# A gated delta rule on one core: the state as the stationary operand, keys and queries as the moving one, and a turn back by transposition

## The chip, the cores and the metric

The kernel runs on one core of a Trainium2 chip. The metric is the device time of one execution in microseconds. Three timed runs of the kernel before gave 3100.2, 3089.31 and 3093.5 us; their median is 3093.5 us. One more execution was taken with the hardware profiler. It took 3072.88 us, of which the profile's span covers 3071.2 us, so that 1.7 us lie around the span. All durations below come from this profiled execution.

## What is computed

The reference is a sequence of two blocks over x of shape 8 x 512 x 256, all in float32: a gated recurrence with an MLP, a mixture of experts (8 experts, top 2, and a shared one), then the layer that the change touches, and last an attention over the half of the tokens that a router chooses. The layer that matters is a gated delta rule with 8 heads, keys of 128 and values of 64:

```python
def step(state, inp):                       # state: batch, head, 64 values, 128 keys
    q_t, k_t, v_t, a_t, b_t = inp
    retained = jnp.einsum('bhvk,bhk->bhv', state, k_t)
    ...
    state = a4 * (state - b4 * rk) + b4 * vk
    o_t = jnp.einsum('bhvk,bhk->bhv', state, q_t)
    return (state, o_t)
```

Before this step come projections of x, a causal convolution of width 4, a SiLU and a normalization of q and k; behind it a gated RMS norm and a projection.

## The kernel before

The kernel runs its stages one behind the other: the first block, the experts, the delta rule, the attention. The function `delta_rule` does the third. It doesn't step through the 512 tokens one by one. For each batch element (8) and each half of the heads (`hg`, 0 or 1, four heads each) it forms a **group**; there are 16 groups, and each treats its 512 tokens in four blocks (`t`) of 128. Inside a block the recurrence is a triangular system; `prepare` (L918, L920) forms its matrices, `inverses` (L948 to L1058) inverts them for a whole group in place, and only the state between blocks is carried on by steps in order.

These steps are the generator `advance`. For the blocks t = 1, 2, 3 of a group, that is 48 times in all, it first reads the old state with the keys and the queries of the block (L1122, tile `pkq`), scales the result by the decay on VectorE (L1124, tile `old`) and takes the part for the keys from the right side `r` (L1125). Then, for every block: `pw` (L1129) applies the inverse to `r`, ScalarE copies it to `w` (L1131), `pst` (L1140) makes the update of the state, which VectorE adds (L1144), and `pow` (L1148) gives what goes into the output `o` (L1152). The tile `state` holds 128 keys on the partitions and 4 heads x 64 values; `kq` holds 128 key channels on the partitions, and for each head the 512 tokens of k and then of q.

In L1122 the operand that is loaded into the array (stationary) is a 128 x 128 piece of `kq`, and the one that streams through it (moving) is the 128 x 64 state of a head. There are 2 x 4 such products in a step. In float32 each product is two instructions on TensorE, each with a weight load of its own.

A group isn't done alone. While group n is advanced, the matrices of group n+1 are formed and inverted, the channels of group n+2 are projected, convolved and normalized (`channels` L848 to L853, `norms` L866 to L885, `fade` L896 to L903), the gates of group n are made (`silus`, L1096 to L1098), a later batch element is loaded (`load`), and the result of group n is normed and projected (`outputs`, L1160 to L1181). Each of these is a generator, and the string `order` says whose next piece is written down: `a` is `advance`, `p` is `prepare`, `i` is `inverses`, `c` is `channels`, `g` is `silus`, and so on. From what is written down in this order, the tile framework's scheduler settles the order of the instructions on each engine. On the chip each engine goes through its own list in that order and waits where an operand isn't there.

The accumulation tiles of `advance` (`pkq`, `pw`, `pst`, `pow`) share the PSUM pool `pq` with two buffers. `old` has two buffers in the pool `un`.

Two places of `inverses` stand near the end of a group's advance and matter below. VectorE ends the inversion of the small blocks with `inv`; ScalarE copies it to `cols` (L986); VectorE transposes that to `dn` (L935); TensorE makes `pn` from it (L1003, 64 products of 32 x 32 blocks); VectorE turns `pn` into `join` (L1004); and TensorE makes `pd` of `join` and `up` (L1009), from which the rest of the inversion follows. These lines belong to the next group, but stand on the same engines.

Of the kernel before, what the change touches and what calls it, by code (L numbers as in the profile page):

```python
# [14 lines left out]
F32 = mybir.dt.float32  # L15
# [5 lines left out]
P = 128  # L21
# [10 lines left out]
H1, VD = 8, 64  # L32
HG = 4
# [4 lines left out]
def bc(ap, axis, n):  # L38

    ap = ap.unsqueeze(axis)  # L40
    shape = list(ap.shape)
    shape[axis] = n
    return ap.to_broadcast(shape)
# [3 lines left out]
def block(ctx: ExitStack, tc: tile.TileContext, a: dict, out: bass.AP):  # L47
    nc = tc.nc
    V, S, G, TE = nc.vector, nc.scalar, nc.gpsimd, nc.tensor
# [4 lines left out]
    def cst(shape, name):  # L54
        return const.tile(shape, F32, name=name, tag=name)

    ident = cst([P, P], "ident")
# [708 lines left out]
    def delta_rule():  # L766
        with ExitStack() as cx:
# [334 lines left out]
            def advance(s):  # L1102


                b, hg, hs, dec, NQ = s.b, s.hg, s.hs, s.dec, s.NQ
                state = None
                for t in range(NT):
                    ts = slice(t * P, (t + 1) * P)
                    r = s.r[t]

                    def sv(tag, **kw):
                        return un.tile([P, HG, VD], F32, name=f"{tag}{b}_{hg}_{t}", tag=tag, **kw)

                    def ps_sv(what):
                        return pq.tile([P, HG, VD], F32, name=f"{what}{b}_{hg}_{t}", tag="pq")

                    old = None
                    if state is not None:
                        ps = pq.tile([P, 2, HG, VD], F32, name=f"pkq{b}_{hg}_{t}", tag="pq")
                        for n in range(2):  # L1120
                            for h in range(HG):
                                TE.matmul(ps[:, n, h, :], s.kq[:, h, n, ts], state[:, h, :], start=True, stop=True)  # L1122
                        old = un.tile([P, 2, HG, VD], F32, name=f"old{b}_{hg}_{t}", tag="old")
                        V.tensor_mul(old, ps, bc(bc(dec[:, 0, t, hs], 1, 2), 3, VD))  # L1124
                        V.tensor_sub(r, r, old[:, 0, :, :])  # L1125
                        yield
                    ps = ps_sv("pw")
                    for h in range(HG):
                        TE.matmul(ps[:, h, :], NQ[:, 0, t * HG + h, :], r[:, h, :], start=True, stop=True)  # L1129
                    w = sv("w")  # L1130
                    S.copy(w, ps)  # L1131
                    yield
                    new = None
                    if t < NT - 1:
                        new = sv("state")
                        if state is not None:
                            G.tensor_mul(new, state, bc(dec[:, 2, t, hs], 2, VD))
                        ps = ps_sv("pst")
                        for h in range(HG):
                            TE.matmul(ps[:, h, :], s.K[t][:, h, :], w[:, h, :], start=True, stop=True)  # L1140
                        if state is None:
                            V.tensor_copy(new, ps)
                        else:
                            V.tensor_add(new, new, ps)  # L1144
                        yield
                    ps = ps_sv("pow")
                    for h in range(HG):
                        TE.matmul(ps[:, h, :], NQ[:, 1, t * HG + h, :], w[:, h, :], start=True, stop=True)  # L1148
                    if state is None:
                        S.activation(s.o[:, t, :, :], ps, AF.Copy, scale=-1.0)  # L1150
                    else:
                        V.tensor_sub(s.o[:, t, :, :], old[:, 1, :, :], ps)  # L1152
                    yield
                    state = new
# [73 lines left out]
            def group(n):  # L1228
# [6 lines left out]


            order = """
                p v t p v p l a v p t l a v p a p a p l a p a p a i l a i g a i c l g i a a e i l a g i e c i a a i l e g e
                i c o i l c o c i o c i l c o i o c i o l i c o i i c o n o n c c n
            """.split()  # L1240

            def seats():
# [44 lines left out]
            with ExitStack() as px:  # L1287
# [5 lines left out]
                for k in first:  # L1293
                    if k not in work:
                        if k in "76":
                            work[k] = shared(next(left), sht, pp, po)
                        elif k in "cneCNE":
                            n = 0 if k in "cne" else 1
# [18 lines left out]
            un = late[0] = cx.enter_context(tc.tile_pool(name="c_un", bufs=2, side="right", reuse_waits="tile"))  # L1317
            pt_ = cx.enter_context(tc.tile_pool(name="c_pt", bufs=2, space=PSUM, reuse_waits="tile"))
            pq = cx.enter_context(tc.tile_pool(name="c_pq", bufs=2, space=PSUM, reuse_waits="tile"))
# [7 lines left out]
            for n in range(total):  # L1327
                s, s1 = groups.pop(n), groups.get(n + 1)
                work = {"v": sides(s), "g": silus(s), "a": advance(s), "o": outputs(s)}
                if s1 is not None:  # L1330
                    work |= {"p": prepare(s1), "i": inverses(s1)}
                if n % 2 == 0 and coming is not None:
                    work["t"] = coming
                elif n + 3 < total:
                    work["l"] = coming = load(n // 2 + 2)
                else:
                    coming = None
                for k in order:
                    if k in "cne" and n + 2 < total and k not in work:
                        if "t" in work:  # L1340
                            drain(work["t"])
                        if n + 2 not in groups:
                            groups[n + 2] = group(n + 2)
                        work[k] = {"c": channels, "n": norms, "e": fade}[k](groups[n + 2])
                    if k in work:
                        next(work[k], None)
                        if n >= total - 2 and k != "p" and groups_done(work, n):
                            steps_ += 1
                            if steps_ % 3:
                                next(sitting, None)  # L1350
                work.pop("l", None)
                drain(*work.values())
            drain(sitting)

    delta_rule()
    kept.close()

# [268 lines left out]
```

## Time and profile before

| what | us |
|---|---|
| median of three timed runs | 3093.5 |
| the profiled execution | 3072.88 |
| its span | 3071.2 |
| TensorE busy in the span | 2884.1 |
| VectorE busy | 1850.4 |
| ScalarE busy | 1587.0 |
| first `pkq` to last `pkq` | 1572.5 to 2722.5 |
| from one group's first `pkq` to the next one's, mean of the 15 distances | 75.0 |

A busy share says how long an engine had an instruction in work. For TensorE it is too high, since products follow each other in a pipeline and the ends are modelled; the time from the start of one instruction to the start of the next is the better measure. The chain of work that ended last follows the time back from the last instruction through what released each one; its shares say which engine set the end. The windows view gives the busy time of every engine in stretches of time, and the timeline lists instructions in order, with the idle time before each and what ended it in square brackets.

### The profile page before, as it was taken

How to read it: one execution, taken by the hardware profiler on the slowest of the kernel's cores; microseconds unless marked ns; L12 is line 12 of the kernel's file. 1: busy time of each engine (PE TensorE's matmuls, PEld its weight loads, DVE VectorE, ACT ScalarE, POOL GpSimd, SP SyncE). 2: the span in 40 equal slices, each digit the busy share in tenths (PEclk: the TensorE clock that was granted, in tenths of full speed). 3: DMA queues.
4: the chain of work that ended last, by engine and by line, in shares of the span. 5: the costliest groups of instructions: out<-in, count | busy, mean ns of one | idle time of the engine just before them, and what ended most of it. 6: DMA issues, size and time to landing. Idle time of an engine off the chain costs nothing.

```text
span 3071.2 us, 59437 instructions
## 1 busy us (share of the span) xinstructions
PE 2884.1 (94%) x24598; PEld 2140.5 (70%) x24598; DVE 1850.4 (60%) x4322; ACT 1587.0 (52%) x2839; POOL 534.1 (17%) x653
## 2 busy tenths in 40 slices
PE   7999999999999999998899999999999999869997
PEld 4565556557999999995466666666666666756774
DVE  5555554545555555556756778687877776654442
ACT  4545453222333333334666677777777776744432
POOL 1000000530100100103111212121212111341111
PEclk9999999999999999999999999999999999769997
DMA  1500001524888888882000001000000000131112
GB/s 69 171 14 28 14 7 26 200 70 152 326 335 331 326 327 331 326 308 76 15 9 1 27 4 29 2 29 2 29 2 26 2 9 22 41 109 57 44 37 66
DMA packets 101406, 307.15 MB, mean 100 GB/s; under 512 B 12680, under 2 KB 83728, under 8 KB 91920
## 3 DMA queue, kind: packets, MB, share of 16 engines
q0 software_dynamic: 19440, 221.19, 19.0%
q1 hardware_dynamic: 79776, 79.80, 7.8%
q8 instruction: 193, 3.16, 0.4%
q10 hardware_dynamic: 1920, 2.37, 0.2%
q14 instruction: 77, 0.63, 0.1%
HBM read 253.25 MB, written 50.08 MB: 99 GB/s over the span
## 4 chain that ended last, share of the span: by engine, by line
PE 74%; DVE 11%; DMA 5%; issue 5%; ACT 4%; POOL 2%; POOLq 0%; DVEq 0%; ACTq 0%
PE p_r L492 15%; PE pc L848 6%; PE p_s L492 5%; PE pp L336 4%; PE pyr L650 4%; PE pj L443 4%; PE pk L918 3%; PE pf L437 3%; DMA w<-in_experts,wrow 3%; PE pkq L1122 2%; DVE cy L852 2%; PE st L1500 2%; PE py L1180 2%; PE pys L535 1%; PE sc L1479 1%
## 5 line engine op out<-in xcount | busy, mean ns | idle before, releaser
L492 PE MATMUL p_r<-zT,w 128*128 128x128 f32 x4544 | 533.3, 275 | 5.4 <-DMA w<-in_experts,wrow 4.8
L492 PEld LDWEIGHTS p_r<-zT,w 128*128 128x128 f32 x4544 | 525.2, 192 | 11.0 <-issue 6.2
L852 DVE SCALAR_TENSOR_TENSOR cy<-pc,conv,cy 128x511 f32<-128x511 f32 (+2 forms) x480 | 351.9, 741 | 137.9 <-ACT cy L850 133.9
L496 ACT ACTIVATE t_r<-p_r,w 128x128 f32<-128x128 f32 x568 | 171.1, 374 | 266.8 <-PE p_r L492 177.0
L492 PE MATMUL p_s<-sxT,shared_w 128*128 128x512 f32 x512 | 231.3, 604 | 3.4 <-ACT sxT L132 1.2
L497 DVE SCALAR_TENSOR_TENSOR l_r<-p_r,w,t_r 128x128 f32<-128x128 f32 x284 | 79.9, 344 | 178.7 <-PE p_r L492 178.7
L492 PEld LDWEIGHTS p_s<-sxT,shared_w 128*128 128x128 f32 x512 | 97.1, 193 | 120.5 <-issue 98.7
L632 POOL DMA_INDIRECT w<-in_experts,wrow x71 | 67.0, 944 | 654.4 <-ACT sg_r L505 634.2
L848 PE MATMUL pc<-cxT,wq 128*128 128x512 f32 x256 | 145.7, 690 | 2.8 <-DVE cy L852 2.5
L336 PE MATMUL pp<-hT,win 128*128 128x512 f32 x320 | 145.6, 609 | 0.1
L497 DVE SCALAR_TENSOR_TENSOR g_r<-p_r,w,t_r 128x128 f32<-128x128 f32 x284 | 80.0, 344 | 98.6 <-PE p_r L492 98.6
L1481 DVE TENSOR_REDUCE maxs<-sc 128x2 f32<-128x512 f32 x128 | 79.4, 683 | 99.0 <-PE sc L1479 99.0
L650 PE MATMUL pyr<-w,htr 128*128 128x256 f32 x568 | 135.5, 382 | 2.1 <-DVE htr L510 2.1
L850 ACT ACTIVATE cy<-pc,conv 128x512 f32<-128x512 f32 x160 | 108.7, 685 | 43.4 <-PE pc L848 41.2
L848 PE MATMUL pc<-cxT,wk 128*128 128x512 f32 x256 | 128.5, 610 | 2.3 <-DVE cy L852 1.8
L918 PE MATMUL pk<-kq 128*128 128x256 f32 x512 | 127.2, 384 | 0.9 <-DVE NQ L920 0.9
L920 DVE SCALAR_TENSOR_TENSOR NQ<-pk,nbk,e 128x256 f32<-128x256 f32 x256 | 110.9, 477 | 27.9 <-PE pk L918 26.6
L505 ACT ACTIVATE sg_r<-g_r 128x512 f32<-128x512 f32 x71 | 44.8, 631 | 158.1 <-DVE g_r L503 158.1
L437 PE MATMUL pf<-hT,fc 128*128 128x512 f32 x256 | 122.4, 604 | 0.0
L443 PE MATMUL pj<-pj,sT 128*128 128x256 f32 x512 | 113.1, 379 | 0.0
L336 PEld LDWEIGHTS pp<-hT,win 128*128 128x128 f32 x320 | 60.8, 195 | 74.6 <-issue 63.3
L650 PEld LDWEIGHTS pyr<-w,htr 128*128 128x128 f32 x568 | 103.1, 191 | 13.5 <-issue 2.3
(406 smaller groups left out, 5958.4 us busy)
## 6 DMA issues: line engine op xcount, KB each, us to landing
zt<-zbuf SPq DMA_DIRECT2D x71, 128.0 KB
ybuf<-yt SPq DMA_DIRECT2D x71, 128.0 KB
zbuf<-zeros SPq DMA_DIRECT2D x11, 768.0 KB
x<-in_x SPq DMA_DIRECT2D x8, 512.0 KB
xbuf<-x SPq DMA_DIRECT2D x8, 512.0 KB
sx<-xbuf SPq DMA_DIRECT2D x8, 512.0 KB
xbuf<-sx SPq DMA_DIRECT2D x8, 512.0 KB
cx<-xbuf SPq DMA_DIRECT2D x8, 512.0 KB
```

Source lines behind the costliest of these rows:

```text
L336: TE.matmul(ps, win[:, k, m : m + P], hT[:, k, :], start=k == 0, stop=k == DK - 1)
L437: TE.matmul(ps, fc[:, k, f * P : (f + 1) * P], hT2[:, k, :], start=k == 0, stop=k == DK - 1)
L443: TE.matmul(ps, sT[:, f, t * P : (t + 1) * P], pj[:, f, :], start=f == 0, stop=f == 7)
L492: last_of[0] = TE.matmul(ps[:, f, :], wx[:, k, (f0 + f) * P : (f0 + f + 1) * P], xin[:, k, :], start=k == 0, stop=k == DK - 1)
L496: S.activation(t3[:, f, :], p3[:, f, :], AF.Identity, bias=b3[:, f0 + f : f0 + f + 1])
L497: V.scalar_tensor_tensor(t1[:, f, :], p1[:, f, :], b1[:, f0 + f : f0 + f + 1], t3[:, f, :], ALU.add, ALU.mult)
L650: last_of[0] = TE.matmul(ps, hT[:, f, :], w2[:, f, :], start=f == 0, stop=f == 3)
L848: TE.matmul(ps, w[k][:, n * P : (n + 1) * P], xT[:, k, :], start=k == 0, stop=k == DK - 1)
L850: S.activation(y, ps, AF.Copy, scale=conv[:, at + n, 3:4])
L852: V.scalar_tensor_tensor(y[:, j:], ps[:, : T - j], conv[:, at + n, 3 - j : 4 - j], y[:, j:], ALU.mult, ALU.add)
L918: TE.matmul(pk[:, j, :, :], kq[:, h + j, 0, ts], kq[:, h + j, :, ts], start=True, stop=True)
L920: V.scalar_tensor_tensor(NQ[:, :, t * HG + h + j, :], pk[:, j, :, :], s.nbk[:, t, h + j : h + j + 1], bc(e[:, h + j, :], 1, 2), ALU.mult, ...
```

## The change

In a step with an old state, the operands change places. The 128 x 64 state of a head is loaded into the array, and the keys and queries of the block, 2 x 128 tokens, are moved through it. Since a state has 64 columns, two heads stand side by side: the even head in the columns 0 to 63 and the odd one in 64 to 127, and their results lie on the partitions 0 to 63 and 64 to 127 of the same PSUM tile. So there are 4 products in the place of 8. The result comes out turned, with values on the partitions and tokens along the row. ScalarE copies it to a new tile `oldT` (128 x 512), and four transpositions on TensorE bring it back, into a second PSUM tile `pold`, from which VectorE makes `old` as before. The step has one `yield` more, between the copy and the transpositions. `oldT` has one buffer, and `old` has one where it had two. Each step takes two buffers of the pool `pq` in turn where it took one.

The string `order` has three `a` more for a group, for the three added yields.

```diff
                     if state is not None:
-                        ps = pq.tile([P, 2, HG, VD], F32, name=f"pkq{b}_{hg}_{t}", tag="pq")
+                        ps = pq.tile([P, 2, 2, P], F32, name=f"pkq{b}_{hg}_{t}", tag="pq")
+                        for h in range(HG):
+                            at = slice(h % 2 * VD, h % 2 * VD + VD)
+                            TE.matmul(ps[at, h // 2, :, :], state[:, h, :], s.kq[:, h, :, ts], start=True, stop=True)
+                        oldT = un.tile([P, 2, 2, P], F32, name=f"oldT{b}_{hg}_{t}", tag="oldT", bufs=1)
+                        S.copy(oldT, ps)
+                        yield
+                        ps = pq.tile([P, 2, HG, VD], F32, name=f"pold{b}_{hg}_{t}", tag="pq")
                         for n in range(2):
-                            for h in range(HG):
-                                TE.matmul(ps[:, n, h, :], s.kq[:, h, n, ts], state[:, h, :], start=True, stop=True)
-                        old = un.tile([P, 2, HG, VD], F32, name=f"old{b}_{hg}_{t}", tag="old")
+                            for c in range(2):
+                                TE.transpose(ps[:, n, 2 * c : 2 * c + 2, :], oldT[:, c, n, :], ident)
+                        old = un.tile([P, 2, HG, VD], F32, name=f"old{b}_{hg}_{t}", tag="old", bufs=1)
                         V.tensor_mul(old, ps, bc(bc(dec[:, 0, t, hs], 1, 2), 3, VD))
                         V.tensor_sub(r, r, old[:, 0, :, :])
                         yield
...
             order = """
-                p v t p v p l a v p t l a v p a p a p l a p a p a i l a i g a i c l g i a a e i l a g i e c i a a i l e g e
-                i c o i l c o c i o c i l c o i o c i o l i c o i i c o n o n c c n
+                p v t p v p l a v p t l a v p a p a p a l a p a p a i l a i a g a i c l g i a a e i l a g i a e c i
+                a a i l e g e i c o i l c o c i o c i l c o i o c i o l i c o i i c o n o n c c n
             """.split()
```

## The prediction

> **What bounds the kernel now.** I read the page first, for the shares of the engines and of the chain; then the windows of 10 us over one pair of groups; then the chain in that pair; then the timeline where the chain leaves TensorE.
>
> ```profile
> PE 2884.1 (94%) x24598; PEld 2140.5 (70%) x24598; DVE 1850.4 (60%) x4322; ACT 1587.0 (52%) x2839; POOL 534.1 (17%) x653
> PE 74%; DVE 11%; DMA 5%; issue 5%; ACT 4%; POOL 2%; POOLq 0%; DVEq 0%; ACTq 0%
> ```
>
> Over the span TensorE bounds. That is an average over stages, and the change touches the delta rule alone, so I look there. The columns are the stretch, its length, the busy time of PE, PEld, DVE, ACT and POOL, the granted clock and the DMAs. One pair of groups: the odd one (heads 4 to 7) has its first `pkq` at 1805.7, the even one at 1877.9, the next odd one at 1953.7.
>
> ```profile
> 1820.00:1830.00 10.00, 10.00 (x56) 7.05 (x54) 8.71 (x17) 8.81 (x12) 4.01 (x4) 1.00 0.00 0
> 1830.00:1840.00 10.00, 7.90 (x288) 5.84 (x286) 9.27 (x19) 8.51 (x13) 0.73 (x1) 0.83 0.02 5
> 1890.00:1900.00 10.00, 9.63 (x57) 7.24 (x58) 9.83 (x29) 4.12 (x8) 6.06 (x9) 1.00 0.10 26
> 1900.00:1910.00 10.00, 9.36 (x159) 5.24 (x157) 10.00 (x17) 9.40 (x13) 5.24 (x6) 1.00 0.10 28
> 1910.00:1920.00 10.00, 8.36 (x264) 5.11 (x266) 9.41 (x22) 9.60 (x15) 1.94 (x2) 1.00 0.12 31
> ```
>
> In the odd group TensorE is full until about 1831 and then stands for some 2 us. In the even group VectorE is full from 1890 to 1910, and ScalarE behind that. So TensorE bounds the steps of the odd group; time saved on it in the even group is saved beside a full VectorE. The chain says the same, and prices two bursts (start, us, what):
>
> ```profile
> 1805.91 1.73 PE pkq L1122 x16
> ...
> 1861.14 1.00 PE pn L868 x16
> ...
> 1886.85 2.01 PE pkq L1122 x16
> 1888.88 0.69 DVE old L1124
> 1891.24 0.69 issue
> 1892.62 0.75 DVE cx L1214
> ```
>
> Behind the second `pkq` of the even group the chain runs on VectorE until 1914.7.
>
> The tail of a group's advance, odd group (start, us, engine, line, in brackets the idle time and what ended it):
>
> ```profile
> 1830.01 0.63 ACT L986 COPY cols<-inv 128x256 f32<-128x256 f32 x1
> 1830.66 0.71 DVE L935 STREAM_TRANSPOSE dn<-cols 128x512 f32<-128x512 f32 x1 [1.65 <-ACT cols L986]
> 1834.16 0.47 DVE L1004 SCALAR_TENSOR_TENSOR join<-pn,second,unit 128x256 f32<-128x256 f32 x1
> 1834.75 0.38 PEld L1009 LDWEIGHTS pd<-join,up 32*32 32x32 f32 x16 [2.15 <-ACT up L992]
> ```
>
> Here a serial path of the inversion, `cols`, `dn`, `pn`, `join`, `pd`, goes from engine to engine. TensorE finishes its last `pow` just before `pn` can begin, then has nothing but this path.
>
> **What is removed and added on TensorE.** A step loses the 16 instructions of 1.73 us. It gains 8 instructions of 256 columns, two heads side by side. No row shows two columns of heads; the nearest is `pn` (L868), 16 instructions of 256 columns in four column strips: 1.00 us, with four starting within 0.02 us of each other, so four rounds, and entering and leaving the strip form is in it. Eight instructions by twos are four rounds as well: 1.00 us. If the two didn't run side by side, it would be eight at the 0.215 us that a 256-column instruction of `pk` takes from start to start, 1.72 us. I take 1.00, since the strips of L868 use the same 128 rows and the same kind of tile, and keep 1.72. The four transpositions follow each other as `ptk` (L1084) does, first start 1868.35, next operation at 1868.78: 0.43 us. Sum: 1.73 - 1.00 - 0.43 = 0.30 us freed in a step, 48 x 0.30 = 14.4 us if TensorE bounded everywhere.
>
> The Trainium skill, page "TensorEngine Tiling (Array Packing)", section "Theoretical Speedup", gives up to twice for one dimension of 64 or less. By that the burst would be an estimated 0.87 us in place of 1.00, and 6 us more would be freed. The row of L868 has the switches in it, so I stay with the row.
>
> **What is added elsewhere.** ScalarE gets 48 copies of 128x512 out of PSUM; `nrow` (L871) is that copy: 587 ns, 28.2 us in all. The compiled lists also have 13 loads of activation tables fewer (272 for 285), at 1283 ns each 16.7 us. So ScalarE gets 11.5 us more. VectorE keeps its `old` (688 ns) and `r` (423 ns). The same page, section "PSUM Bottleneck", speaks against the change: tiling makes TensorE faster but not the emptying of PSUM, which may become the bound. By that rule each step pays 0.59 us for 0.30 us, an estimated loss of 14 us; the trace says only where ScalarE has room for it, so I go by place.
>
> **The wait that is added** is that of the transpositions for `oldT`, and of what is queued behind them. The path from the last round of `pkq` to `old` was one pipeline end; it becomes the end of a 256-column product (0.42 to the copy), the copy 0.59, 0.25 to the first transposition, 0.33 for four, 0.33 to VectorE. In steps 1 and 2 the compiled order puts 0.9 to 1.7 us of other products between `pkq` and the transpositions, which just covers it. Where ScalarE is late (the odd group's second copy lies behind two `own` copies of 1.08 us and a table load) I count 0.3 us of standing, and 0.6 us more where `r` comes late for `pw`. That is the 0.9 us that three steps free in the odd group: zero there. In the even group VectorE bounds, and it gets the same work: zero too.
>
> **Step 3 decides.** Before, the last `pw` and `pow` of a group lie ahead of `pn`, each with a product of 0.86 us or more to hide the copy `w`. In the compiled order after, the third set of transpositions comes so late that they lie inside `pn`: 13 of its 64 products, `pw`, 20 products, `pow`, 31 products, then `pd`. `pd` must wait for all. Counted from the end of `dn`: `r` 0.41 and 0.27 until `pw` starts, 1.76 from a `pw`'s start to the product behind its copy (1809.69 to 1811.45), `pow` 0.89, a switch of form 0.09 and 31 products 0.51, 0.2 until `join`, `join` 0.47, 0.05: 4.65 us to `pd`. Before it is 3.41 us in the odd group (1831.37 to 1834.78) and 2.81 in the even one (1908.12 to 1910.93). That is 1.2 us and 1.8 us later. In the odd group ScalarE takes up `pd` only at 1838.60, 1.95 us after its end, behind a table load; in the new order its copies come straight behind, so those 1.2 us are made up. In the even group ScalarE takes `pd` at once (1912.18) and is full from there, so the 1.8 us stay, and VectorE stands in front of the last `o`, in the stage where it bounds. Eight even groups: 14.4 us. `dn` itself I leave where it is: VectorE has `r` and `o` (0.8 us) no longer ahead of it, but the new `old` is, in part.
>
> At the end of the stage, two groups have little beside them, and the path of a step is 0.6 us longer (2.6 for 1.99 us, `pkq` to `old`, from the pieces above): six steps, less where queues hide it, 2.5 us.
>
> **Sum:** 14.4 + 2.5 = 17 us: 3090 us on the profiled execution of 3072.9 us. The median of the timed runs is 3093.5, 20.6 us above that execution; the same 17 us on it give **3111 us**.
>
> One more unknown is the clock. In 1830 to 1840, where TensorE stands for 2 us, 0.83 was granted: half speed for 3.4 us. More standing there may bring one such stretch to every group, up to 1.7 us x 16 = 27 us; or the freed standing elsewhere takes some away. I take zero and keep +27 for the range.
>
> **Rivals.**
> 1. *TensorE bounds in practice, and the freed time arrives* (the side where it gets faster): the scheduler's covers hold, and the tail's 1.2 to 1.8 us fall into the 1.5 to 2.1 us in which TensorE stands before `pd` anyway. For it: 74% of the chain; against it: the full VectorE of the even groups. It decides if `pd` comes no later after `dn` than now. 14.4 - 2.5 = 12 us less: 3081 us.
> 2. *A wash:* odd groups gain 0.9 x 8 = 7 us, even groups lose about as much. 3093 us.
> 3. *The heads don't run side by side,* so the change doesn't do what it says: 0.72 us more in each step; 24 steps in odd groups, where TensorE bounds, 17 us, on top of the 17: 3128 us.
>
> **Chances.** Forecast 0.50, rival 1 0.25, rival 2 0.19, rival 3 0.06. The forecast's own range is 3100 to 3125. Range: rival 1 with a little more at the low end, 3077; 3111 with the clock's 27 us at the high end, 3138. A measurement of this kernel tells about 0.3% (9 us) from no change. Faster by more: rival 1, 0.25. Slower by more: the forecast and rival 3, less a little of the forecast's low end, 0.55. Within: 0.20.
>
> **What would show it.** Four starts of `pkq` rounds 0.215 us apart, each of two instructions within 0.02 us, and a burst of about 1.0 us: side by side. A wait of `pd` for `join` that grows above 2.1 us, and `pw` and `pow` standing inside `pn`, show the tail. VectorE's `o` waiting for `pow` in even groups shows where it lands. The distance of two odd groups' first `pkq`, 148 to 150 us now, should grow by 2 us. The forecast is wrong if this distance shrinks, and its mechanism is wrong if `pd` follows `dn` within 3 us.

## The result, and the profile after

The changed kernel takes 3108.23 us (median of 5 runs, 3100.64 to 3116.53) beside 3094.5 us of the kernel before on the same chip (5 runs, 3089.31 to 3100.2): a ratio of 1.0041, 95% interval 1.0026 to 1.0056, so 13.7 us slower. A second comparison on another chip gave 1.0069 (1.0051 to 1.0086), 22.9 us slower. The forecast was 3111 us. All ratios below are against runs of the kernel before on the same chip; the medians of before on the chips used differ by up to 18 us. One run of `tail_both`, 3705.66 us, lay in a slower state of the chip and is not in its ratio.

The page after: busy time by engine, then the chain by engine.

```profile
PE 2907.4 (94%) x24406; PEld 2111.7 (68%) x24406; DVE 1839.9 (59%) x4322; ACT 1597.5 (51%) x2874; POOL 534.5 (17%) x653
PE 75%; DVE 7%; ACT 6%; issue 4%; DMA 4%; POOL 3%; another core or an unknown queue 0%; POOLq 0%; SPq 0%; DVEq 0%; ACTq 0%
```

TensorE issues 192 matmul instructions fewer (48 x (8 + 4 - 16)) and yet is busy 23 us longer (6 us in the later profiles used below, 2900.0 for 2893.9). ScalarE gets 10.5 us more (11.5 were forecast).

The chain, in an odd group (first `pkq` at 1815.54), through step 3 and the tail:

```profile
1840.07 0.45 PE pold L1129 x4
...
1840.55 0.69 DVE old L1131
1841.24 0.63 DVE dn L935
...
1841.91 0.42 PE pn L1003 x26
1842.34 1.05 PE pw L1136 x8
1843.39 0.47 PE pn L1003 x39
1843.85 1.11 PE pow L1155 x8
...
1844.99 0.43 DVE o L1159
...
1845.44 1.07 ACT oq L1167
1846.51 1.86 PE pd L1009 x93
```

`pw` and `pow` stand inside `pn`, as the compiled order had it, and `pd` follows the end of `dn` by 4.6 us. New to the prediction are the first two DVE lines: `dn` stands behind the third `old`. And `pd` takes 1.86 us in the chain; from its first to its last start it is 1.69 us, for 1.02 in the undisturbed groups before. The windows of the same stretch (PE, PEld, DVE, ACT, POOL, granted clock, DMAs) say why:

```profile
1830.00:1840.00 10.00, 10.00 (x49) 6.17 (x50) 6.83 (x13) 8.71 (x13) 3.67 (x4) 1.00 0.01 2
1840.00:1850.00 10.00, 7.92 (x304) 6.93 (x303) 8.07 (x15) 5.43 (x9) 0.72 (x1) 0.75 0.01 3
1850.00:1860.00 10.00, 8.96 (x154) 4.88 (x153) 6.96 (x17) 9.60 (x16) 0.00 (x0) 0.90 0.01 2
```

0.75 over one 10 us, 0.90 over the next: 2.5 and 1.0 us lost, so some 7 us at half speed (6.8 in the clock's records), twice the 3.4 us of the dip shown before. In this kernel every group from the third to the thirteenth has 6.8 us at half speed. In the chain `pd` is let go by the end of `oq`; `join` (1845.87, 0.48 us) had ended 0.15 us sooner.

The first profile of before lay 21.6 us under the median of its runs, so what follows compares two later profiles from one chip (spans 3083.4 and 3095.2 us). Means over four even and four odd groups, from the first `pkq` at 1876.7 to that at 2477.3 before and from 1882.1 to 2496.5 after, in us:

| | even, before | even, after | odd, before | odd, after |
|---|---|---|---|---|
| first `pkq` to the end of `dn` | 30.24 | 29.08 | 25.64 | 26.34 |
| end of `dn` to `pd` | 2.82 | 4.71 | 3.41 | 4.64 |
| `pd` to the next group's `pkq` | 43.86 | 43.93 | 44.20 | 44.91 |
| sum | 76.92 | 77.71 | 73.25 | 75.89 |
| of it at half speed | 4.27 | 6.83 | 4.27 | 6.83 |

A pair is 3.4 us longer: 0.8 us in the even group, 2.6 us in the odd one. This is the price in the middle of the stage. From the first `pkq` of the stage to the last, the same two profiles differ by 19.2 us (1158.3 and 1177.5), and their spans by 11.8 us, for the 22.9 us between the medians timed on this chip. Half of the added time at half speed is 2.6 us a pair.

TensorE's waits from 1800 to 2560 in the same two profiles (line waited for, us in total, times, longest), first before, then after:

```profile
PE pd L1009 <- DVE join L1004: 16.4, 9, 2.1
...
PE pu L1033 <- ACT n L1028: 1.9, 6, 0.4
```

```profile
PE pn L1003 <- DVE dn L935: 10.7, 10, 1.5
PE pw L1136 <- DVE r L1132: 7.8, 9, 1.5
PE pu L1033 <- ACT n L1028: 5.2, 5, 1.0
PE pd L1009 <- ACT oq L1167: 4.8, 7, 0.7
...
PE pd L1009 <- DVE join L1004: 2.0, 3, 0.7
```

The waits ahead of `pd` went from 16.4 us (for `join`) to 6.8 us (for `oq` and `join`), and 18.5 us of waits for `dn` and `r`, which before doesn't show, stand in their place. So one sign that the prediction named, a wait of `pd` for `join` above 2.1 us, did not come: `pd` is later, but `pn`, `pw` and `pow` fill the time ahead of it, and TensorE stands earlier, for `dn` and `r`. From the first `pkq` of a step to the start of `old` it is 3.0 to 5.6 us in the middle groups, for 1.9 to 2.3 us before.

### The profile page after: what moved, and what is told of

Read it like the earlier page. It is cut to its first block, busy times and chain, and to the rows that moved or that the text cites. A ratio compares the mean times of both kernels' runs of the same rounds, so it can differ in the third digit from the quotient of the medians.

```text
span 3107.9 us, 59080 instructions
## 1 busy us (share of the span) xinstructions
PE 2907.4 (94%) x24406; PEld 2111.7 (68%) x24406; DVE 1839.9 (59%) x4322; ACT 1597.5 (51%) x2874; POOL 534.5 (17%) x653
## 4 chain that ended last, share of the span: by engine, by line
PE 75%; DVE 7%; ACT 6%; issue 4%; DMA 4%; POOL 3%; another core or an unknown queue 0%; POOLq 0%; SPq 0%; DVEq 0%; ACTq 0%
PE p_r L492 15%; PE pc L848 7%; PE p_s L492 6%; PE pp L336 4%; PE pyr L650 4%; PE pj L443 4%; PE pk L918 3%; PE pf L437 3%; DMA w<-in_experts,wrow 2%; PE pw L1136 2%; PE pow L1155 2%; PE st L1507 2%; PE py L1187 2%; PE sc L1486 1%; PE pys L535 1%
## 5 line engine op out<-in xcount | busy, mean ns | idle before, releaser
L852 DVE SCALAR_TENSOR_TENSOR cy<-pc,conv,cy 128x510 f32<-128x510 f32 (+2 forms) x480 | 353.1, 742 | 117.5 <-ACT cy L850 113.1
L920 DVE SCALAR_TENSOR_TENSOR NQ<-pk,nbk,e 128x256 f32<-128x256 f32 x256 | 112.3, 476 | 28.9 <-PE pk L918 27.5
```

The costliest lines, as they stand in the source:

```text
L852: V.scalar_tensor_tensor(y[:, j:], ps[:, : T - j], conv[:, at + n, 3 - j : 4 - j], y[:, j:], ALU.mult, ALU.add)
L920: V.scalar_tensor_tensor(NQ[:, :, t * HG + h + j, :], pk[:, j, :, :], s.nbk[:, t, h + j : h + j + 1], bc(e[:, h + j, :], 1, 2), ALU.mult, ...
```

## Experiments

Theory A is that of the prediction: the lateness of `pd` in the even groups is the loss. Rivals formed on the way: B, every group pays for the longer path through ScalarE; C, the odd groups lose it; D, the granted clock; E, TensorE's new waits for `dn` and `r`; F, any rearrangement of the old order costs this much.

**New form in one kind of group.** `even_only`:

```diff
-                    if state is not None:
+                    if state is not None and hg == 0:
...
-                for k in order:
+                for k in order_new if n % 2 == 0 else order_old:
```

> The new form in the even groups (hg 0) alone, with the order string of after there; the odd groups (hg 1) have the old form and the old string, and the tile old has one buffer everywhere. The compiled order of the even groups' last step is that of after (13 products of pn, pw, 20, pow, 31, pd), that of the odd groups is that of before. Theory A (the prediction: the loss is the tail of the even groups, odd groups gain and lose nothing): nearly the whole loss, 13 us over before, 3107 us. Rival B (every group pays about 0.9 us, for the longer path through ScalarE): half of it, 7 us, 3101 us. Rival C (the odd groups lose it, since TensorE's freed time there goes into waits and into one more stretch of half clock): 0 to 3 us, 3095 to 3098 us.

`odd_only` has `hg == 1` and `n % 2 == 1`.

> The mirror of it: the new form in the odd groups alone, with the order string of after there, the old form and string in the even groups. Its even groups compile as in before; in its odd groups the scheduler puts the third set of transpositions, pw and pow behind pn and pd, so pd waits for none of them. Theory A: no loss, 3092 to 3097 us (the last odd group pays some 1 us). Rival B: half of the loss, 7 us, 3101 us. Rival C: all of it, 3105 to 3108 us, if the loss doesn't hang on the order of pw, pow and pn; if it does, this run is at before as well.

Measured: even_only 1.0049 (1.0034 to 1.0063), 14.8 us between the medians; odd_only 1.0074 (1.0047 to 1.0100), 21.6 us. For even_only alone A was right (13 us); but A expected no loss of odd_only, where `pd` follows `dn` by 2.6 to 2.8 us in the middle even groups, as in before. Each half alone costs about as much as the whole. They don't add up, so no theory that gives each group a price of its own (A, B, C) stands as it was. Even_only is a clean half by its compiled order. Odd_only isn't: every second odd group has an order of its own (`pd` ahead of `pw` and `pow`), the others end as in after, and in some of its even groups the last `pw` and `pow` stand at other places than in before.

**The tail by itself.** `tail_even` moves one `a` one place to the left:

```diff
-                p v t p v p l a v p t l a v p a p a p a l a p a p a i l a i a g a i c l g i a a e i l a g i a e c i
+                p v t p v p l a v p t l a v p a p a a p l a p a p a i l a i a g a i c l g i a a e i l a g i a e c i
```

> The changed kernel with one piece of the order string moved by one place (the transpositions of block 1 are written down one piece earlier). In the compiled order this takes pw and pow of the last step out of pn in all even groups but the first and the last: pkq, four products, the transpositions, three, pw, one, pow, then all 64 products of pn and pd. Odd groups stay as in after. Theory A: the even groups' 1.8 us come back, 6 or 7 times 1.8 is 11 to 13 us: 3095 to 3098 us. Rival B: the path through ScalarE is as long as before, 3106 to 3109 us. Rival C: no change from after either, 3108 us. If the clock's stretches of half speed are what costs, they should become fewer in the even groups alone.

`tail_both` moves the last pieces of `advance`:

```diff
-                p v t p v p l a v p t l a v p a p a p a l a p a p a i l a i a g a i c l g i a a e i l a g i a e c i
-                a a i l e g e i c o i l c o c i o c i l c o i o c i o l i c o i i c o n o n c c n
+                p v t p v p l a v p t l a v p a p a p a l a p a p a i l a i a g a a i a a c l g i a a e i l a g
+                i e c i i l e g e i c o i l c o c i o c i l c o i o c i o l i c o i i c o n o n c c n
```

> The changed kernel with the last pieces of advance written down earlier in the order string, so that in the compiled order pw and pow of the last step lie ahead of pn in both kinds of groups; there is no product between pw and pow, so TensorE stands there for the copy w, about 0.9 us more than with cover. Theory A: even groups get 1.8 us back and lose 0.9, odd groups lose 0.9 and gain 1.2 that they don't need: 8 x 0.9 less than after and 8 x 0 to 0.9 more, 3101 to 3108 us. Rival B: 3108 us. Rival C (odd groups pay for the split of pn): some 10 us less, 3096 to 3100 us.

Measured: tail_even 1.0106 (1.0084 to 1.0128), the slowest of all; tail_both 1.0050 (1.0032 to 1.0068), about as after. In tail_both `pw` and `pow` lie ahead of `pn`, but `pd` still follows `dn` by 3.7 us in the even groups and 4.5 us in the odd ones, so it tells little. In tail_even `pd` does follow `dn` by 2.94 us in the even groups in place of 4.7, as A wanted, and then TensorE stands behind it (timeline of PE, in brackets the wait and what ended it):

```profile
2070.47 1.04 PE L1009 MATMUL pd<-join,up 32*32 32x32 f32 x50 [1.03 <-DVE join L1004]
2072.43 1.01 PE L1009 MATMUL pd<-join,up 32*32 32x32 f32 x44 [0.92 <-issue]
...
2075.90 0.86 PE L1016 MATMUL pu<-up,join 32*32 32x32 f32 x46 [1.33 <-issue]
...
2087.21 1.96 PE L848 MATMUL pc<-cxT,wq 128*128 128x512 f32 x4 [1.83 <-ACT cy L850]
```

From `pd` to the next group it is 47 to 49 us there, for 43.9 after, and most of these groups have 10.2 to 13.7 us at half speed, for 6.8. The 1.8 us are won and more than given back. The clock takes a large part: tail_even's mean clock is 0.9457, for 0.9538 of before on that chip. By odd_only A falls as an account of the whole loss. That a `pd` placed sooner brings nothing by itself is not shown by tail_even, since what follows it changed as well.

**The clock.** Both kernels once more, unchanged, for profiles near their medians.

> The changed kernel unchanged, beside the others of this set on one chip. 8 to 18 us over before (ratio 1.0026 to 1.0056 so far). In its profile: some 6.8 us of half speed in most groups, as in the first profile of it.

> The kernel before, once more, for a second profile. No difference beyond 0.3%. Theory D (since formed from the profiles: the stage's time less half of its time at half speed is 1088 us before and 1090 to 1095 us in all five changed kernels, so what differs is how long the clock stays at half speed): if this profile lies near the median, 15 to 20 us above the first one, it has some 30 to 40 us more at half speed than the 116 us of the first, and again some 1088 us net. Theory A (the tail): the time of the groups doesn't follow the clock.

Measured: after_again 1.0069 (1.0051 to 1.0086); before_again 1.0000 (0.9985 to 1.0015), with 146 us at half speed in the stage for 116 us in the first profile, and 1085 us net for 1088 (the stage's time less half of its time at half speed), as D had it. Then two products whose result nobody reads, in after (`after_fill2`) and in before (`before_fill2`):

```diff
                 pd = bank("pd4")
+                flat = dn.rearrange("p i x -> p (i x)")
+                for _ in range(2):
+                    TE.matmul(pd.rearrange("p u x -> p (u x)"), flat[:, 0:128], flat, start=True, stop=True)
```

> The changed kernel with two products more in every group whose result nobody reads: ahead of the products of pd, 128 x 512 each, into the bank that pd then overwrites, moved while TensorE waits for join. The order of everything else around pd stays. They take 4 x 0.43 us at full speed, and the wait that they lie in is 0.7 to 1.5 us, so pd comes 0.2 to 1.0 us later. Theory D: TensorE's quiet stretch around pd no longer sends the clock to half speed, or for one window of 3.4 us in place of two; 13 groups x 1.7 to 3.4 us, less 3 to 16 us of delay: 10 to 40 us faster than after_again. Theory A or B (the serial path counts): 3 to 16 us slower than after_again.

> The same two products in the kernel before, where the wait for join is 2.1 us, so that they fit in without delay. Theory D: the half speed behind the wait goes, 3 to 10 us in a group, at half its length: 10 to 40 us faster than before. Theory A or B: 0 to 5 us slower than before.

Measured: after_fill2 1.0094 (1.0073 to 1.0114), before_fill2 1.0010 (0.9997 to 1.0023). No gain, so D's forecast of 10 to 40 us failed in both. The clock did rise, as the mean over the profiled execution shows, first before_again, then before_fill2:

```profile
core 0: 3083.4 us, clock 0.952
```

```profile
core 0: 3073.2 us, clock 0.966
```

Half speed in the stage went from 146 to 72 us (before) and from 175 to 113 us (after), yet the timed difference to the unfilled kernels is +3.6 and +6.0 us. So the clock's gain was spent, and not in the same way in the two kernels. In after, `pd` follows `dn` by 7.3 us in most groups, for 4.7: that is more than the 4 x 0.43 = 1.7 us filled in. In before, `pd` is hardly later (3.17 us for 2.81 in the even groups, 3.30 for 3.41 in the odd ones), but the compiled order of the odd groups changed ahead of it, and there `dn` ends 27.65 us after the first `pkq`, for 25.64. So neither run is the kernel with nothing but a higher clock.

What the clock is worth can be estimated in three ways, and they don't agree. The filling itself is 16 x 4 x 0.43 = 27.5 us of TensorE; if just that is lost, 24 and 22 us came back through the clock. Half of the time no longer spent at half speed is 37 and 31 us. And over the 88 runs of before in all four sets, time and mean clock go together (correlation -0.86), 28.6 us for 0.01 of clock; the clock's mean rose by 0.010 and 0.008, which by that is 27 and 22 us. But within the 23 runs on this chip alone it is 17.9 us for 0.01 (correlation -0.89; 21 to 27 on the other three chips), which gives 17 and 14 us. That a higher clock goes with a shorter time is shown; its price lies somewhere between 18 and 29 us for 0.01, and what the filling cost is not measured apart.

**Which blocks, the string, and the turn back.** `steps12`, the new form in blocks 1 and 2 alone, the old one in block 3 (one `a` fewer in the string):

```diff
-                    if state is not None:
+                    if state is not None and t < NT - 1:
```

> The new form in blocks 1 and 2 of every group alone; block 3 has the old form, so one yield and one piece of the order string go, and in the compiled order pw and pow of the last step lie ahead of pn with products between them, as before. Theory E (formed from the two kernels' second profiles: the change does take 2.5 us of work from TensorE in a pair of groups, but TensorE stands longer, 2.5 us for dn, which comes behind the third old on VectorE, 2.2 us for r ahead of pw, and 0.9 us go to half speed): the wait for dn goes, about 1.7 of the 2.5 us of work stay freed, and the waits for r shrink; 5 to 14 us faster than before. The prediction's view (steps 1 and 2 gain nothing, step 3 costs 14 us): as before, within 5 us. Rival F (whatever is altered, the scheduler's new order costs 10 to 20 us, since the old order was fitted to the old pieces): 10 to 20 us slower than before.

`no_turn`, the products without the way back, so that `old` takes the values of other tokens:

```diff
-                        oldT = un.tile([P, 2, 2, P], F32, name=f"oldT{b}_{hg}_{t}", tag="oldT", bufs=1)
-                        S.copy(oldT, ps)
                         yield
-                        ps = pq.tile([P, 2, HG, VD], F32, name=f"pold{b}_{hg}_{t}", tag="pq")
-                        for n in range(2):
-                            for c in range(2):
-                                TE.transpose(ps[:, n, 2 * c : 2 * c + 2, :], oldT[:, c, n, :], ident)
+                        ps = ps.rearrange("p c n f -> p (c n f)").rearrange("p (n h v) -> p n h v", n=2, h=HG)
```

> The changed kernel without the turn back: oldT, its copy and the transpositions are left out, and VectorE takes old straight from the turned product (so the values of old are those of other tokens). The order string and the yields are those of after. TensorE loses 0.95 us of work in every step against before (1.78 to 0.83 us by the starts), ScalarE gets no copy, and the path to old is shorter than before. Theory E, if TensorE bounds everywhere: 45 us faster than before; if the even groups' VectorE hides theirs, 20 to 25 us. Rival F: 45 or 25 us less 10 to 20 us.

`string_only`, the kernel before with after's string and

```diff
+                        yield
-                        old = un.tile([P, 2, HG, VD], F32, name=f"old{b}_{hg}_{t}", tag="old")
+                        old = un.tile([P, 2, HG, VD], F32, name=f"old{b}_{hg}_{t}", tag="old", bufs=1)
```

> The kernel before with the order string of after, a bare yield where after has its new one, and one buffer for old: the pieces are written down where after has them, and no operation is new. The tail of the even groups compiles as before, that of the odd ones nearly so. Theory E: within 5 us of before. Rival F: 10 to 20 us slower than before, as after itself.

Measured on one chip: steps12 1.0023 (1.0006 to 1.0039), no_turn 0.9954 (0.9938 to 0.9971), string_only 1.0025 (1.0007 to 1.0043). Steps12 and string_only lie between E and F, no_turn where F had it. The string with its single buffer costs some 8 us by the ratio, 3.4 us between the medians, without any new operation. The products, side by side and not turned back, bring 14 us against before and some 17 to 22 us against string_only. How much work that is, the starts on TensorE say. The old burst takes 1.73 us from its first start to the next operation. The new one takes 1.01 us, and the operation ahead of it 0.09 us more, since the array changes its form: from the last `pk` to the first `pkq` it is 0.309 us, for 0.216 before. That is 0.62 us less in a step, or 48 x 0.62 = 30 us (the 0.95 us of the expectation counts the four rounds alone, without the change of form). As timed, half of it arrives against before, and over half against string_only. Part of the rest went to the clock: no_turn's mean is 0.9496, for 0.9523 of before and 0.9521 of string_only on that chip. And the way from no_turn to after, 0.9 to 1.2% or 27 to 35 us, is the price of the turn back (over chips; after didn't run in this set). That is more than its 48 x 0.44 = 21 us of TensorE. Steps12 has no gain either: its blocks 1 and 2 take about 4 x 0.19 = 0.8 us of work from TensorE in a pair, but their waits remain (its waits of TensorE, 1800 to 2560):

```profile
PE pd L1009 <- DVE join L1004: 19.0, 10, 2.2
PE pw L1145 <- DVE r L1132: 7.7, 9, 1.5
PE pn L1003 <- DVE dn L935: 4.5, 4, 1.1
```

The wait for `r` is as long as in after (7.7 and 7.8 us) though the third step is the old one: in both kernels it stands in step 2 of the middle groups.

**The turn back off the path.** `turn_aside`:

```diff
+                        left = ps.rearrange("p c n f -> p (c n f)").rearrange("p (n h v) -> p n h v", n=2, h=HG)
                         ps = pq.tile([P, 2, HG, VD], F32, name=f"pold{b}_{hg}_{t}", tag="pq")
...
-                        V.tensor_mul(old, ps, bc(bc(dec[:, 0, t, hs], 1, 2), 3, VD))
+                        V.tensor_mul(old, left, bc(bc(dec[:, 0, t, hs], 1, 2), 3, VD))
```

> The changed kernel with all its work, but with the turn back off the path: ScalarE copies oldT and TensorE makes the four transpositions into pold as in after, and nobody reads pold; VectorE takes old straight from the turned product (so its values are those of other tokens, as in no_turn). It tells the work of the turn back (0.44 us of TensorE, 0.59 us of ScalarE in a step) from its place in the path to old, r and pw. No_turn is 0.46% faster than before (14 us), after 0.4 to 0.7% slower, so the turn back costs 27 to 35 us. If the work is what costs (48 x 0.44 us of TensorE, and the products' 0.95 us a step brought half of its sum): 10 to 21 us over no_turn, 4 us faster to 7 us slower than before. If the path is what costs: within 5 us of no_turn, 9 to 15 us faster than before. If ScalarE's copies are what costs, or the two together: 10 us slower than before or more, as after.

Measured: 1.0056 (1.0035 to 1.0078), as slow as after, and at the mean clock of before (0.9518 and 0.9515), so that here the clock isn't the reason. This speaks against the path alone as the cause, but the experiment isn't clean: the scheduler made yet another order, with new waits for ScalarE, `pc` for `cy` 7.3 us and `pd` for `oq` 3.0 us in the same 760 us. Whether the turn back costs by its work or by its waits stays open.

## Why the forecast came out, and where its steps were wrong

The total was right, and the direction; the places and several of the prices were not. That the total came out is in good part luck.

**Side by side: right.** The starts come in pairs 0.007 us apart, in four rounds 0.21 to 0.27 us apart. A burst is 1.01 us, 1.00 forecast, and the transpositions 0.44 for 0.43. The entering of the new array form, 0.09 us, lies ahead of the burst, and so it does ahead of the row of L868 (`pto` to `pn` is 0.202 us, `pto` to `pto` 0.109); the forecast took it to be inside the 1.00 us. So a step frees 1.73 - 1.01 - 0.09 - 0.44 = 0.19 us, where 0.30 was forecast. The Trainium skill's page "TensorEngine Tiling (Array Packing)", section "Theoretical Speedup", would have made the burst an estimated 0.87 us; the measured 1.01 us is nearer to the row of L868.

**"pd follows dn by 4.65 us": right,** 4.64 and 4.71 us, though the parts are off by up to 0.2 us and make up for each other, and the last release is `oq`, which the sum didn't have. **"In the even group the 1.8 us stay": wrong in the sum.** The 1.9 us are there, but `dn` itself comes 1.2 us sooner after the group's first `pkq`, in the part that was set to zero: there `inv` ends 26.5 us after it, for 27.6. An even group loses 0.8 us, 8 of them 6 us, for 14.4 forecast.

**"Those 1.2 us are made up" in the odd group: wrong.** ScalarE takes up `pd` 1.97 us after its start, for 3.8 before, as forecast. But with `pow` late, `o`, `oq` and the norm's `oms` are late as well: `oms`, with its table load and the load that follows it for `kq`, now falls between the second and the third copy of `pd`, where before it lay ahead of them. Timeline of ScalarE, first before, from `up` to the copies of `pu` (`pd` at 1834.78), then after (`pd` at 1846.50):

```profile
1833.93 1.28 ACT L1166 ACT_TABLE_LOAD   x1
...
1836.77 1.28 ACT L853 ACT_TABLE_LOAD   x1 [1.15 <-DVE cy L852]
...
1838.60 1.74 ACT L1011 COPY half<-pd 32x512 f32<-32x512 f32 x3
...
1841.87 2.33 ACT L1018 COPY NQ<-pu 32x512 f32<-32x512 f32 x4
```

```profile
1848.47 1.16 ACT L1011 COPY half<-pd 32x512 f32<-32x512 f32 x2 [1.97 <-PE pd L1009]
...
1850.31 1.28 ACT L1173 ACT_TABLE_LOAD   x1
...
1851.84 0.58 ACT L1011 COPY half<-pd 32x512 f32<-32x512 f32 x1
1852.43 1.28 ACT L853 ACT_TABLE_LOAD   x1
...
1855.39 2.32 ACT L1018 COPY NQ<-pu 32x512 f32<-32x512 f32 x4
```

From `pd` to the copies of `pu` it is 8.9 us for 7.1. Nothing is made up; 0.7 us more are lost behind `pd`.

**"`dn` itself I leave where it is": wrong in the odd group.** There `inv` ends sooner, and `dn` later. Timeline of VectorE and ScalarE before (first `pkq` at 1805.7), then after (at 1815.5):

```profile
1827.62 0.68 DVE L975 TENSOR_REDUCE inv<-pl 128x64 f32<-128x512 f32 x1
...
1827.92 1.28 ACT L853 ACT_TABLE_LOAD   x1
```

```profile
1835.12 0.67 DVE L975 TENSOR_REDUCE inv<-pl 128x64 f32<-128x512 f32 x1
...
1836.92 1.28 ACT L853 ACT_TABLE_LOAD   x1
...
1838.75 0.57 ACT L1124 COPY oldT<-pkq 128x512 f32<-128x512 f32 x1
1839.21 0.63 ACT L853 ACTIVATE kq<-cy 128x512 f32<-128x512 f32 x1
1839.74 0.62 ACT L986 COPY cols<-inv 128x256 f32<-128x256 f32 x1
```

From the first `pkq`, `inv` ends after 20.3 us, for 22.6 before, but ScalarE takes up `cols` after 24.2 us in both: two table loads and then `oldT` and `kq` stand ahead of it. So the 2.3 us by which `inv` is sooner are lost on ScalarE, some 0.5 us of them to `oldT`. On VectorE `dn` then stands behind `old`, which waits 3.58 us for `pold`, and this makes it 0.7 us later in the group than before:

```profile
1840.55 0.69 DVE L1131 TENSOR_TENSOR old<-pold,dec 128x512 f32<-128x512 f32 x1 [3.58 <-PE pold L1129]
1841.16 0.70 DVE L935 STREAM_TRANSPOSE dn<-cols 128x512 f32<-128x512 f32 x1
```

In the even group it is `r` in step 2 that the forecast had covered: `pw` waits 0.8 to 1.5 us for it in the middle groups (0.56 us in the odd group, where 0.6 was forecast).

So neither the added wait nor ScalarE's added copies were free where the forecast took zero. The same page of the skill, section "PSUM Bottleneck", warned of the emptying of PSUM; the prediction's estimate by it was a loss of 14 us. The sign agrees. The places seen here are the copy's turn on ScalarE and that of `old` on VectorE; no run here shows ScalarE as the bound as a whole (51% busy).

**"One more unknown is the clock. I take zero": wrong.** From the third group to the thirteenth, every group now has two windows of 3.4 us at half speed, where before it had none to three. On the chip of the second comparison the mean clock is 0.9500 after and 0.9554 before; at 28.6 us for 0.01 that is 15 of the 22.9 us, at the 17.9 us of this chip's own runs 10. The text gave up to 27 us for this case and left it out of the sum. By half of the added time at half speed it is 2.6 of a pair's 3.4 us. So the sum reached the right size by luck, with 14.4 us from a place that gave 6, and zero from a term that gave some 10 to 15. The price of the clock rests on a correlation, and a longer stand of TensorE can cause both a longer time and a lower clock, so this is an estimate, not a proof. And the clock isn't all: odd_only, tail_both, string_only and turn_aside are 8 to 20 us slower than the 88 runs of before would be at the same clock.

**The rivals.** No wash and no gain. The heads do run side by side. Rival 1 had `pd` come no later after `dn`; it comes 1.2 to 1.9 us later. And freed time doesn't simply arrive: in no_turn 30 us of work are gone and 14 us are won.

What costs the rest is open: the runs show longer waits for `dn` and `r`, a cost of the order string with its single buffer alone, and a lower clock, but no run takes away one of them without changing another.

## What to carry to other kernels

Swapping the operands to fill the array pays only if the result can stay turned: here the products alone won 14 us of the 30 us of work they saved, and turning back cost 27 to 35 us, more than the transpositions' own 21 us. When an order was found for the old pieces, a new piece has to be followed on every in-order queue that it joins, here `oldT` ahead of `cols` on ScalarE and `old` ahead of `dn` on VectorE, and a wait that moves must be followed to the next work that depends on it. And where TensorE stands or moves little for some microseconds, look at the granted clock behind it before calling the stretch off the path.

## What the runs showed of the hardware

The clock falls and rises on a fixed grid of 3.413 us in these traces. If the columns moved in each such window are counted, each by the share of the 128 x 128 array that its tile covers, then in the first profiles of before and after (1500 to 2700) all 34 windows at full speed that were followed by half speed had moved at most 1,216, and none that was followed by full speed less than 1,152; a window full of large products moves 3,400 to 4,100 (matmuls counted by their start). In the other runs the border is less sharp: by the same count, windows of up to 1,792 were followed by half speed (tail_even), so this is a rule of thumb from these traces and no threshold. The 32 x 32 products of the inversion count for little in this measure: `pn`, `pd` and `pu` keep TensorE busy, and most of the falls come where they stand. In the first profile of before, the window from 1978.2 holds 128 of `pn` and 8 of `pow` without any wait of TensorE, 640 columns by the count, and half speed followed; no wait of TensorE between 1800 and 2560 in the later profiles was longer than 2.1 us. In the middle of the stage after's pair of groups fell into step with the grid: 153.6 us, 45 windows, so its pairs show the same dips over and over, while the pairs of before drift against it (148.4 to 152.4 us). And one piece of the order string moved by one place cost about as much as the whole change: tail_even is 1.06% above before, after 0.41 and 0.69%.
